# Attention of the later images: values as products with queries on partitions, and whole scan ticks beside it

## The chip, the cores and the metric

The kernel runs on one core of a Trainium2 chip, in float32 throughout. The metric is the device time of one execution in microseconds (us), lower is better. Five instruction streams run side by side on the core, each in its own program order: TensorE (PE in the profile; its weight loads are PEld), VectorE (DVE), ScalarE (ACT), GpSimd (POOL) and the queue that issues DMAs (SP). They wait for each other by semaphores only.

## The reference

Four layers, each added to its input, each on a group-normalised copy of it. `x` has 4 images of 128 channels and 64 x 64 = 4096 pixels.

```
x = x + attention(gn(x))     # q, k, v by 128x128 matrices; softmax over all 4096 pixels
x = x + conv5x5(gn(x))       # weights built from two radial tables
x = x + scan(gn(x))          # two directions: h = exp(delta*A)*h + delta*x*B ; y = C.h + D*x
x = x + conv3x3(gn(x))
```

The part of the attention that the change rewrites is

```
scores = einsum('bic,bjc->bij', q, k) * scale
attn   = softmax(scores, axis=-1)
out    = einsum('bij,bjc->bic', attn, v)
```

The kernel takes the exponential of the scores without subtracting a maximum, sums the exponentials for each query, and divides at the end. If a sum falls out of a wide range a second program with maxima runs; with these inputs it does not run.

## The kernel before, in words

**Two streams of work.** The state-space scan of layer 3 is cut into ticks: `scan_core` has 256 for each image, 1024 in all. A tick handles 128 rows (32 channels by 4 states) over 1024 pixels. Its steps are `drive` (L1387, POOL: input times B, written to `db`), `decay` (L1372, ACT: exp(delta*A) into `da`, which lies in PSUM), `recur` (L1392, DVE: the scan instruction over `da` and `db`; then, on some ticks, the product with C into `hc`), `weigh` (L1418, POOL: that product on the other ticks), `keep` (L1410 and on, ACT: saves the last state) and `collect` (L1423, PE: sums over states into `y`). All else, namely each image's attention, 5x5 convolution, scan operands, and at the end the output convolutions, is a Python generator, `images()`, that issues a few instructions and yields what they are thought to cost.

**What sets the order.** The order is written out at build time. After each half of a tick, a credit grows by half of `PACE` (2.74 us), and the generator is asked for pieces until the credit is spent (L1709 to L1719). So beside the scan of image 0 the front (attention, convolution, operands) of image 1 is issued, and so on; beside the scan of the last image the output convolutions of the first three, at `ENDPACE`. Engines take their instructions in that order and run ahead only within it.

**Half ticks and whole ticks.** PSUM has eight banks. `s`, `a`, `z` and `y` hold one each. Four more are lent either to the pool `s2`, which holds a second score bank and three `da` tiles of 512 columns, or to the pool `wide`, which holds two `da` tiles of 1024. `widen` (L1652) decides: beside a convolution, and at the end, ticks are whole (one decay, one scan, one product with C of 1024 columns); beside attention and operands they are halved (two of each, of 512 columns). `to_pool` (L1329) gives POOL every third product with C in whole ticks and two of five in half ticks beside the attention.

**Attention before.** `attention` (L467) takes blocks of 512 queries, 8 for an image, against 32 tiles of 128 keys: 256 units `u`. In each, `scores` makes one 128x512 score tile in bank `s` or `s2` (keys on partitions), ACT writes its exponential to one of 8 slots of `ring`, and `values`, two units later, multiplies `v` (the weights) with that slot into `acc` (L524), channels on partitions. Once for every four units `sums` (L546) adds the exponentials over keys by four narrow matmuls with ones into `zp`. At a block's end the sums go out to DRAM and back so as to stand as a row on every partition (`spill` to `stage_rows`), and `settle` (L661) multiplies, adds bias and input, and takes a sum for the next normalisation, on DVE. The first image runs without a scan beside it and takes its sums on DVE and POOL instead (`side_sums`).

Of the kernel before, what the change touches and what calls it, by code (L numbers as in the profile page):

```python
# [32 lines left out]
P = 128  # L33
# [3 lines left out]
MM = 512  # L37
# [8 lines left out]
PRODUCT, HOP, SLOT, PACE, ENDPACE, AHEAD = 0.86, 1.7, 0.7, 2.74, 1.5, 4  # L46
# [6 lines left out]
def conv_preact_kernel(  # L53
# [366 lines left out]
    def attention_start(b, xn):  # L420
# [10 lines left out]
        v = v[:, : NJT * C].rearrange("p (j c) -> p j c", c=C)  # L431
# [7 lines left out]
        def keys(i):  # L439

            tag = "saz"[i % 3] if b == 0 else "s" if i < 3 else ("s", "s2")[i % 2]
            pvs[i] = bank(tag, f"pv_{b}_{i}").rearrange("p (t c) -> p t c", c=C)
            for t in range(TPM):
                nc.tensor.matmul(
                    pvs[i][:, t, :], xn[:, bass.ts(i * TPM + t, P)], wv, start=True, stop=True
                )

        def take(i):
            nc.scalar.copy(v[:, i * TPM : (i + 1) * TPM, :], pvs.pop(i))
# [17 lines left out]
    def attention(b, xs, xn, v, st, safe, loads):  # L467

        ring = exchange(b).rearrange("p (r m) -> p r m", m=MM)
        later = {}  # L470
        rq, acc, zp, mb = {}, {}, {}, {}
# [5 lines left out]
        def queries(blk):  # L477
            pr = bank("s", f"pr_{b}_{blk}")
            nc.tensor.matmul(pr, wqk, xn[:, bass.ts(blk, MM)], start=True, stop=True)
            rq[blk] = pools["bg"].tile([P, MM], F32, tag="r", name=f"r_{b}_{blk}")  # L480
            nc.scalar.activation(rq[blk], pr, AF.Identity, bias=bqk)

        def row_max(blk):

            part = small.tile([P, TPM, NM], F32, tag="part", name=f"part_{b}_{blk}")
            for t in range(TPM):
                for k in range(NM):
                    pp = bank("s", f"pmax_{b}_{blk}_{t}_{k}")
                    nc.tensor.matmul(
                        pp, rq[blk][:, bass.ts(t, P)], xn[:, bass.ts(k, MM)],  # L490
                        start=True, stop=True,
                    )
                    nc.vector.tensor_reduce(part[:, t, k : k + 1], pp, AX.X, ALU.max)
            m = small.tile([P, TPM], F32, tag="rmax", name=f"rmax_{b}_{blk}")
            nc.vector.tensor_reduce(m, part, AX.X, ALU.max)
            pb = bank("s", f"pmb_{b}_{blk}")
            spread(pb, m)
            mb[blk] = pools["bg"].tile([P, MM], F32, tag="raw", bufs=1, name=f"mb_{b}_{blk}")
            nc.scalar.copy(mb[blk], pb)

        def spread(dst, cols):

            for t in range(TPM):
                nc.tensor.matmul(
                    dst[:, bass.ts(t, P)], cols[:, t : t + 1].to_broadcast([P, P]), ident,
                    start=True, stop=True,
                )

        def scores(u):
            blk, j = divmod(u, NJT)  # L510
            sc = bank(("s", "s2")[u % 2], f"sc_{b}_{u}")
            nc.tensor.matmul(sc, xn[:, bass.ts(j, P)], rq[blk], start=True, stop=True)  # L512
            pt = ring[:, u % NRING, :]
            if safe:
                nc.vector.tensor_tensor(pt, sc, mb[blk], ALU.subtract)
                nc.scalar.activation(pt, pt, AF.Exp)
            else:
                nc.scalar.activation(pt, sc, AF.Exp)  # L518

        def values(u):  # L520
            blk, j = divmod(u, NJT)
            if j == 0:
                acc[blk] = bank("a", f"acc_{b}_{blk}")
            nc.tensor.matmul(  # L524
                acc[blk], v[:, j, :], ring[:, u % NRING, :], start=j == 0, stop=j == NJT - 1
            )

        due = []  # L530

        def sums_due(u):
            beside = "collected" in ready
            ready.discard("collected")
            if due and due[0][1] <= u and (beside or u >= due[0][2]):
                sums(due.pop(0)[0])
                return PRODUCT
            return 0.0

        def sums(u):  # L540

            blk, j = divmod(u, NJT)
            if j == 3:
                zp[blk] = bank("z", f"zp_{b}_{blk}")
            for g in range(4):
                nc.tensor.matmul(  # L546
                    zp[blk][g * 32 : (g + 1) * 32, :], ones[:, :32],
                    ring[:, (u - 3 + g) % NRING, :], start=j == 3, stop=j == NJT - 1,
                    tile_position=(0, g * 32), skip_group_check=True,
                )  # L550

        state = {}


        fill = pools.get("fill") if not safe else None
        sides = {}
# [11 lines left out]
        def evict_sums(blk):  # L568
            zs = None
            if not fill:  # L570
                zs = pools["bg"].tile([P, MM], F32, tag="zs", bufs=1, name=f"zs_{b}_{blk}")
                nc.scalar.copy(zs, zp.pop(blk))
            elif blk + 1 < NM:
                zs = pools["bg"].tile([P, MM], F32, tag="zs", bufs=1, name=f"zs_{b}_{blk}")
                pz = bank("z", f"pz_{b}_{blk}")
                for g, e in enumerate("dp"):
                    nc.tensor.matmul(
                        pz[g * 32 : (g + 1) * 32, :], ones[:, :32], sides.pop((blk, e)),
                        start=True, stop=True, tile_position=(0, g * 32), skip_group_check=True,
                    )  # L580
                nc.scalar.copy(zs[:64], pz[:64])
            state[blk] = None, zs
# [3 lines left out]
        def spill(blk):  # L586
            raw, zs = state[blk]
            n = 2 if fill else 4
            zd = dram.tile([4, MM], F32, tag="zp", name=f"zd_{b}_{blk}")
            nc.sync.dma_start(zd[:n], zs[0 : n * 32 : 32, :])  # L590
            state[blk] = raw, zd[:n]

        def gather(blk):
            raw, zd = state[blk]
            zt = small.tile([P, 4, RUN], F32, tag="zt", name=f"zt_{b}_{blk}")
            n = zd.shape[0]
            nc.sync.dma_start(zt[:, :n, :], zd.rearrange("g (p j) -> p g j", j=RUN))
            state[blk] = raw, zt[:, :n, :]

        def invert_rows(blk):  # L600
            raw, zt = state[blk]
            z = zall[:, b * NJT + blk * TPM : b * NJT + (blk + 1) * TPM]
            nc.vector.tensor_reduce(z, zt.rearrange("p g j -> p j g"), AX.X, ALU.add)
            zr = small.tile([P, RUN], F32, tag="zr", name=f"zr_{b}_{blk}")
            nc.vector.reciprocal(zr, z)
            state[blk] = raw, zr

        def put_rows(blk):
            raw, zr = state[blk]
            zd = dram.tile([P, RUN], F32, tag="zd", name=f"zi_{b}_{blk}")  # L610
            nc.sync.dma_start(zd, zr)
            state[blk] = raw, zd
# [19 lines left out]
        def turn(blk):  # L632

            raw, zs = state[blk]
            parts = [(zs, zsel)] if zs is not None else [
                (sides.pop((blk, e)), ones[:, 0:1]) for e in "dp"
            ]
            pz = bank("z", f"pz_{b}_{blk}")
            for t in range(TPM):
                for n, (part, add) in enumerate(parts):  # L640
                    nc.tensor.matmul(
                        pz[:, t : t + 1], part[:, bass.ts(t, P)], add,
                        start=n == 0, stop=n == len(parts) - 1,
                    )
            state[blk] = raw, pz

        def invert(blk):
            raw, pz = state[blk]
            z = zall[:, b * NJT + blk * TPM : b * NJT + (blk + 1) * TPM]
            nc.vector.tensor_copy(z, pz[:, :TPM])  # L650
            zr = small.tile([P, TPM], F32, tag="zr", name=f"zr_{b}_{blk}")
            nc.vector.reciprocal(zr, z)
            state[blk] = raw, zr

        def widen_out(blk):
            raw, zr = state[blk]
            pb = bank("z", f"pzb_{b}_{blk}")
            spread(pb, zr)
            state[blk] = raw, pb
# [10 lines left out]

        queries(0)
        ready.add((b, "begun"))
        yield HOP
        HELD = 4
        for u in range(N):
            blk, j = divmod(u, NJT)
            cost = sums_due(u)
            if safe and j == 0:
                row_max(blk)
            scores(u)  # L680
            cost += PRODUCT

            if j == 17 and blk + 1 < NM:
                queries(blk + 1)
                cost += PRODUCT
            w = u - 2
            if w >= 0:
                if w < N - HELD:
                    values(w)
                    cost += PRODUCT  # L690
                d = w % NJT
                if fill:
                    side_sums(w)
                elif d == NJT - 1:
                    sums(w)
                    cost += PRODUCT
                elif d % 4 == 3:
                    due.append((w, u + (3 if d == 3 else 1), u + NRING - 5))
                if d == NJT - 1:
# [9 lines left out]
                    cost += PRODUCT if fill else 0.0  # L709
# [3 lines left out]
            yield cost or HOP  # L713
        for w in (N - 2, N - 1) if fill else ():
            side_sums(w)
        blk = NM - 1

        def taps_to(n):
# [3 lines left out]
            part = kept[:, n * k : min((n + 1) * k, NTAP), :]  # L722
            if not fill and part.shape[1]:
                nc.sync.dma_start(to[:, : part.shape[1], :], part)

        values(N - 4)
        stage_rows(blk - 1, "s")
        yield PRODUCT
# [1072 lines left out]
```

## Time and profile before

| what | value |
|---|---|
| median of 3 runs | 4395.23 us (4394.08 to 4402.77) |
| the profiled execution | 4397.93 us |
| span in its profile, first to last instruction | 4396.1 us |
| busy in the span | PE 3829.8, DVE 3698.7, POOL 3601.9, ACT 2384.6 us |
| first drive of the scan, last drive | 677.4 us, 4322.5 us |

How to read it: the share of the busy time is an average over stages. The page cuts the span into 40 slices of 110 us and gives the busy tenths of each engine:

```profile
PE   8999998999998979999989889999988567575656
PEld 4444433333333333333333333333333112121212
DVE  4832217999998989999989899999989899999996
ACT  3343226666664376666653666666644654545442
POOL 3433308999998979999989899999988799999995
PEclk9999999999999989999999999999999778797877
```

The first six slices are the first image alone; from the seventh on the scan runs. From there to slice 31 three rounds of attention, convolution and operands run beside it, and the last nine slices hold the last image's scan with the output convolutions. A float32 matmul is two passes in the profile, each with a weight load, so counts of PE are twice those of the code. Ends of matmuls are modelled: a pass of 512 columns reads as 592 ns where passes follow each other every 430 ns.

### The profile page before, as it was taken

The page shows a single profiled execution, that of the slowest core. Times are in us where ns is not written, and L with a number is a line of the kernel's source. Part 1 is how long each engine was busy: PE and PEld are TensorE (multiplying, and loading weights), DVE is VectorE, ACT ScalarE, POOL GpSimd, SP SyncE. Part 2 cuts the span into 40 slices and gives each one's busy share as a digit, 9 for nine tenths or more (in the row PEclk, how much of TensorE's full clock was granted, in tenths as well). Part 3 has the DMA queues.
Part 4 walks back from the last instruction along what each step waited for, and adds up shares of the span by engine and source line. Part 5 has one row for each costly group of instructions (what it writes and reads, how often), then busy time and mean ns, then how long its engine had stood idle before and what let it go on. Part 6 is the DMA issues. An engine that isn't in the chain of part 4 may idle for free. (4 is left out here: it accounts for less than half of the span.)

```text
span 4396.1 us, 42164 instructions
## 1 busy us (share of the span) xinstructions
PE 3829.8 (87%) x12828; PEld 1415.9 (32%) x12828; DVE 3698.7 (84%) x3465; ACT 2384.6 (54%) x4331; POOL 3601.9 (82%) x1712
## 2 busy tenths in 40 slices
PE   8999998999998979999989889999988567575656
PEld 4444433333333333333333333333333112121212
DVE  4832217999998989999989899999989899999996
ACT  3343226666664376666653666666644654545442
POOL 3433308999998979999989899999988799999995
PEclk9999999999999989999999999999999778797877
DMA  2120016555555575555555665555555656656562
GB/s 67 45 94 10 3 58 238 184 181 186 176 182 174 180 264 181 178 186 175 181 172 178 213 225 176 194 172 179 173 173 197 237 209 203 226 200 230 181 233 77
DMA packets 241009, 746.40 MB, mean 170 GB/s; under 512 B 44194, under 2 KB 45474, under 8 KB 240516
## 3 DMA queue, kind: packets, MB, share of 16 engines
q1 hardware_dynamic: 238852, 742.88, 49.3%
q8 instruction: 103, 1.69, 0.2%
q14 instruction: 134, 1.10, 0.1%
q10 hardware_dynamic: 1920, 0.73, 0.1%
HBM read 667.82 MB, written 75.69 MB: 169 GB/s over the span
## 5 line engine op out<-in xcount | busy, mean ns | idle before, releaser
L1390 POOL TENSOR_TENSOR db<-dx,br 128x1024 f32<-128x1024 f32 x1024 | 2401.8, 2375 | 225.8 <-DMA dx<-dxd 65.7
L1383 ACT ACTIVATE da<-de,a_neg 128x512 f32<-128x512 f32 (+1 forms) x1635 | 1301.7, 799 | 843.9 <-DVE da L1400 359.2
L512 PE MATMUL sc<-r,x 128*128 128x512 f32 x2048 | 1083.4, 612 | 41.2 <-ACT last L1416 17.1
L524 PE MATMUL acc<-exchange,v 128*128 128x512 f32 x2048 | 1053.5, 596 | 5.2 <-ACT raw L629 1.6
L1421 POOL TENSOR_TENSOR hc<-hc,cr 128x1024 f32<-128x1024 f32 x385 | 914.4, 2375 | 6.5 <-ACT last L1416 4.6
L1403 DVE TENSOR_TENSOR hc<-da,cr 128x512 f32<-128x512 f32 (+1 forms) x1002 | 839.8, 838 | 69.2 <-PE sc L512 1.3
L1400 DVE TENSOR_TENSOR_SCAN da<-da,last,db 128x512 f32<-128x512 f32 (+1 forms) x479 | 859.6, 1795 | 38.0 <-POOL db L1390 28.4
L1439 PE MATMUL y<-hc,sel 128*32 128x512 f32 x4096 | 609.4, 647 | 294.1 <-POOL hc L1421 225.1
L518 ACT ACTIVATE exchange<-sc 128x512 f32<-128x512 f32 x1024 | 601.2, 587 | 394.0 <-PE sc L512 381.2
L512 PEld LDWEIGHTS sc<-r,x 128*128 128x128 f32 x2048 | 362.6, 190 | 648.2 <-issue 357.4
L524 PEld LDWEIGHTS acc<-exchange,v 128*128 128x128 f32 x2048 | 388.2, 191 | 504.7 <-issue 480.2
L1400 DVE TENSOR_TENSOR_SCAN hc<-da,last,db 128x512 f32<-128x512 f32 (+1 forms) x289 | 492.0, 1703 | 8.6 <-POOL db L1390 5.1
L1400 DVE TENSOR_TENSOR_SCAN da<-da,da,db 128x512 f32<-128x512 f32 x363 | 467.0, 1287 | 8.0 <-ACT da L1383 8.0
L566 POOL TENSOR_TENSOR sidep<-sidep,exchange 128x512 f32<-128x512 f32 x120 | 172.0, 1433 | 247.2 <-ACT exchange L518 244.7
L1439 PEld LDWEIGHTS y<-hc,sel 128*32 128x32 f32 x4096 | 114.8, 112 | 734.6 <-POOL hc L1421 316.8
L1400 DVE TENSOR_TENSOR_SCAN hc<-da,hc,db 128x512 f32<-128x512 f32 x248 | 318.1, 1283 | 37.5 <-ACT da L1383 12.9
L566 DVE TENSOR_TENSOR sided<-sided,exchange 128x512 f32<-128x512 f32 x120 | 98.7, 822 | 213.2 <-ACT exchange L518 212.2
L787 PE MATMUL pcm<-xpm,cs 128*128 128x512 f32 x432 | 211.3, 638 | 44.5 <-ACT xpm L392 44.5
L1400 DVE TENSOR_TENSOR_SCAN da<-da,db 128x512 f32<-128x512 f32 (+1 forms) x160 | 240.0, 1500 | 4.5 <-POOL db L1390 2.8
L1416 ACT COPY last<-da 128x1 f32<-128x1 f32 x476 | 73.7, 155 | 275.1 <-DVE hc L1403 273.0
L546 PE MATMUL zp<-exchange,ones 128*32 128x512 f32 x1536 | 205.8, 600 | 0.1
L1039 PE MATMUL pq<-xpe,cs 128*128 128x512 f32 x280 | 134.5, 631 | 39.8 <-ACT xpe L392 39.8
(257 smaller groups left out, 2763.7 us busy)
## 6 DMA issues: line engine op xcount, KB each, us to landing
br<-bm SPq DMA_DIRECT2D x512, 512.0 KB
cr<-cm SPq DMA_DIRECT2D x512, 512.0 KB
de<-dd SPq DMA_DIRECT2D x64, 512.0 KB
dx<-dxd SPq DMA_DIRECT2D x64, 512.0 KB
xs<-in_x_dram SPq DMA_DIRECT2D x16, 512.0 KB
xsd<-xs SPq DMA_DIRECT2D x16, 512.0 KB
xcd<-xc SPq DMA_DIRECT2D x16, 512.0 KB
bm<-bs SPq DMA_DIRECT2D x32, 256.0 KB
```

What stands on the lines that cost most here:

```text
L512: nc.tensor.matmul(sc, xn[:, bass.ts(j, P)], rq[blk], start=True, stop=True)
L518: nc.scalar.activation(pt, sc, AF.Exp)
L524: nc.tensor.matmul(acc[blk], v[:, j, :], ring[:, u % NRING, :], start=j == 0, stop=j == NJT - 1)
L546: nc.tensor.matmul(zp[blk][g * 32 : (g + 1) * 32, :], ones[:, :32], ring[:, (u - 3 + g) % NRING, :], start=j == 3, stop=j == NJT - 1, tile ...
L566: eng.tensor_tensor(s, s, ring[:, u % NRING, :], ALU.add)
L787: nc.tensor.matmul(acc.rearrange("p (r w) -> p r w", w=W), weights[:, t, :], xp[:, y : y + RPM, dx : dx + W], start=t == 0, stop=t == k * ...
L1383: nc.scalar.activation(da, rep["de", b, c, d, g][:, bass.ts(h, size)], AF.Exp, scale=a_neg[:, at(i)])
L1390: nc.gpsimd.tensor_tensor(dbs[i], rep["dx", b, c, d, g], rows["b", b, c, d, q], ALU.mult)
L1400: nc.vector.tensor_tensor_scan(h, da, db[:, cut], before, ALU.mult, ALU.add)
L1403: nc.vector.tensor_tensor(hc[:, cut], h, rows["c", b, c, d, q][:, cut], ALU.mult)
L1421: nc.gpsimd.tensor_tensor(hcs[i], hcs[i], rows["c", b, c, d, q], ALU.mult)
L1439: nc.tensor.matmul(y[r : r + SG, :], sel, hcs[first + gg][:, bass.ts(h, MM)], start=False, stop=q == NQ - 1, tile_position=(0, r), skip_gr ...
```

## The change

The attention of images 1 to 3 is written anew; that of image 0 keeps its way, as `attention_first`.

- **Units.** A unit is now 256 queries by two key tiles: two score matmuls of 256 columns in one bank, one exponential of 512 columns. There are again 256 units for an image, in 16 parts of 256 queries. Score banks are `s` and `z`; `s2` is not used beside attention any more.
- **Values.** The exponentials are the weights (128 keys by 128 queries) and a tile of `v` with a 129th column of ones is what streams: four matmuls of 129 columns for a unit, queries on partitions. The 129th column of `acc` is the sum of the exponentials, so `sums` and the row's way through DRAM go.
- **End of a part.** ACT copies 258 columns out of `acc`, DVE takes reciprocals of two columns, ACT divides two tiles of 128 by a per-partition scale. When two parts are done, `turn` puts the input block into a bank by a product with the identity, adds the four 128x128 tiles turned back by products with the identity, and ACT adds the bias, writes the result and takes its sum.
- **Holding back.** At a part's start `values` of the first unit is held until the second unit's scores are issued (`owed`).
- **Whole ticks.** `widen` goes by a mark `narrow`, set from the end of a convolution to the end of the operands: ticks are whole beside the attention as well.
- **Paces.** 2.65, 2.61, 2.6 and 1.5 for the four images, instead of 2.74 and 1.5; four value matmuls are counted as 0.9.

```diff
-PRODUCT, HOP, SLOT, PACE, ENDPACE, AHEAD = 0.86, 1.7, 0.7, 2.74, 1.5, 4
+PRODUCT, VALUES, HOP, SLOT, AHEAD = 0.86, 0.9, 1.7, 0.7, 4
+PACES = 2.65, 2.61, 2.6, 1.5
...
-        v = v[:, : NJT * C].rearrange("p (j c) -> p j c", c=C)
+        v = v[:, : NJT * (C + 1)].rearrange("p (j c) -> p j c", c=C + 1)
+        nc.gpsimd.memset(v[:, :, C : C + 1], 1.0)
...
+        def scores(u):
+            part, k = divmod(u, NK2)
+            blk, half = divmod(part, 2)
+            cut = bass.ts(half, HM)
+            sc = slots.take("sc")
+            for n in range(2):
+                nc.tensor.matmul(
+                    sc[:, bass.ts(n, HM)], xn[:, bass.ts(2 * k + n, P)], rq[blk][:, cut],
+                    start=True, stop=True,
+                )
+            pt = ring[:, u % NRING, :]
...
+                nc.scalar.activation(pt, sc, AF.Exp)
+
+        def values(u):
+            part, k = divmod(u, NK2)
+            if k == 0:
+                acc[part] = bank("a", f"acc_{b}_{part}")
+            for n in range(2):
+                for t in range(TPH):
+                    nc.tensor.matmul(
+                        acc[part][:, bass.ts(t, CV)],
+                        ring[:, u % NRING, n * HM + t * P : n * HM + (t + 1) * P],
+                        v[:, 2 * k + n, :],
+                        start=(k, n, t) == (0, 0, 0), stop=(k, n) == (NK2 - 1, 1),
+                        skip_group_check=True,
+                    )
+
+        def evict(part):
...
+            nc.scalar.copy(turned[blk][:, cut], acc.pop(part)[:, : TPH * CV])
...
+        def invert(part):
...
+            nc.vector.reciprocal(
+                zall[:, n : n + TPH], rows(blk)[:, half * TPH : (half + 1) * TPH, C]
+            )
+
+        def divide(part):
...
+            for t in range(TPH):
+                row = rows(blk)[:, half * TPH + t, :C]
+                nc.scalar.activation(row, row, AF.Identity, scale=zall[:, n + t : n + t + 1])
+
+        def turn(blk):
+
+            sums[blk] = bank("a", f"po_{b}_{blk}") if blk + 1 == NM else slots.take("po")
+            nc.tensor.matmul(
+                sums[blk], ident, xs[:, bass.ts(blk, MM)], start=True, stop=False,
+                skip_group_check=True,
+            )
+            for t in range(TPM):
+                nc.tensor.matmul(
+                    sums[blk][:, bass.ts(t, P)], rows(blk)[:, t, :C], ident,
+                    start=False, stop=True, skip_group_check=True,
+                )
+            cut = bass.ts(blk, MM)
+            nc.scalar.activation(
+                xs[:, cut], sums.pop(blk), AF.Identity, bias=bv_c, accum_out=st.sum(blk)
+            )
...
+            if u >= 2:
+                owed.append(u - 2)
+            if owed and (owed[0] % NK2 or len(owed) > 1):
+                for w in owed:
+                    values(w)
+                    cost += VALUES
...
-        ready.add((b, "convolved"))
-        ready.discard("convolving")
-        while b > 0 and "wide" in pools:
+        ready.update({(b, "convolved"), "narrow"})
+        while "wide" in pools:
             yield HOP
...
+        ready.discard("narrow")
         ready.add((b, "all"))
...
-                wide = (B - 1, "all") in ready or "convolving" in ready
+                wide = "narrow" not in ready
...
-                if b + 1 == B:
-                    pace = ENDPACE
+                pace = PACES[min(b, len(PACES) - 1)]
```

## The prediction

> **What bounds the kernel now.** The page's chain of waits covers 1% of the span (the last 70 us), so I read in another order: the slices, then busy time by stage, then each engine's own rows and waits in the attention stage. In the slices PE, DVE and POOL all stand near 9 from the eighth slice to the thirty-first; only stages tell which one decides. A stage is cut where the drives (L1390, one a tick) and the attention's matmuls begin and end. Busy time of PE, PEld, DVE, ACT, POOL in the attentions of images 1, 2, 3, in one convolution stage, and beside the last scan:
>
> ```profile
> 723.00:1370.00 647.00, 620.08 (x2300) 223.84 (x2299) 612.54 (x641) 421.80 (x866) 605.41 (x270) 0.99 0.55 185
> 1640.00:2292.00 652.00, 625.91 (x2306) 224.17 (x2305) 615.04 (x643) 423.50 (x872) 602.94 (x267) 0.99 0.54 181
> 2564.00:3218.00 654.00, 624.50 (x2306) 225.09 (x2305) 615.68 (x647) 422.19 (x871) 603.05 (x268) 0.99 0.53 179
> 1370.00:1540.00 170.00, 163.69 (x524) 63.71 (x522) 161.96 (x114) 66.23 (x76) 162.64 (x75) 0.99 0.51 174
> 3496.00:4250.00 754.00, 476.01 (x1503) 144.20 (x1504) 725.36 (x428) 359.26 (x576) 717.06 (x327) 0.79 0.61 214
> ```
>
> The built order has 184 drives in each attention (9 to 193, 262 to 446, 515 to 699), so a tick takes 647/184 = 3.52, 3.54 and 3.55 us. The last stage has nearly the same scan in whole ticks; its drives:
>
> ```profile
> L1390 POOL TENSOR_TENSOR db<-dx,br x255: 2337/2372/2452, 3495.3 to 4317.9; 128x1024 f32<-128x1024 f32 x128
> ```
>
> That is 822.6/254 = 3.24 us a tick. What VectorE runs in a tick, half ticks in the first attention and whole ones in the last stage (count, busy, mean, idle before):
>
> ```profile
> L1403 DVE TENSOR_TENSOR hc<-da,cr 128x512 f32<-128x512 f32 x220 | 152.1, 691 | 14.1 <-PE sc L512 0.4 <-PE acc L524 0.4
> L1400 DVE TENSOR_TENSOR_SCAN da<-da,da,db 128x512 f32<-128x512 f32 x110 | 141.5, 1286 | 0.0
> L664 DVE TENSOR_TENSOR rz<-raw,rz 128x512 f32<-128x512 f32 x7 | 4.8, 680 | 0.0
> ```
> ```profile
> L1400 DVE TENSOR_TENSOR_SCAN da<-da,last,db 128x1024 f32<-128x1024 f32 x112 | 262.2, 2341 | 9.7 <-POOL db L1390 9.7
> L1403 DVE TENSOR_TENSOR hc<-da,cr 128x1024 f32<-128x1024 f32 x156 | 191.0, 1224 | 15.0 <-issue 0.4
> ```
>
> And who VectorE and ScalarE waited for in the first attention:
>
> ```profile
> DVE pzb L664 <- PE pzb L504: 4.7, 1, 4.7
> DVE da L1400 <- ACT da L1383: 2.1, 1, 2.1
> ```
> ```profile
> ACT da L1383 <- DVE da L1400: 119.6, 91, 2.6
> ACT da L1383 <- DVE hc L1400: 50.9, 76, 1.0
> ACT exchange L518 <- PE sc L512: 29.1, 35, 2.8
> ```
>
> VectorE waits for others about 12 us in 647; the other 22 of its 34 idle us are about 0.035 us between each two of 641 instructions. ScalarE waits 170 us for VectorE to free decays. So VectorE sets the attention tick. PE is not full, whatever its 96% says: by pitches (0.43 us a 512-column pass, below) 512 score, 512 value, 128 sum and 184 y pass-times make (512+512+128+184) x 0.43 + 6 for queries = 580 of 647 us, 90%.
>
> **What the Trainium skill says.** "TensorE: Matmul & The Clock Gate", "LDWEIGHTS (loading the stationary operand)", prices a load at its columns over 1.2, 107 ns for 128, and says loads are pulled ahead of running matmuls. This is the point on which the changed products stand: 128 new weights for each 129 columns. The first image's values have that very shape:
>
> ```profile
> L444 PE MATMUL pv<-wv,x x47: 274/275/341, 21.8 to 27.0; 128*128 128x128 f32 x47
> ```
>
> 47 passes begin within 5.2 us: 0.113 us each, with loads whose rows read 0.192 us. The load is hidden. The same page ("What's actually happening") says the idle array runs at half clock; the trace agrees in that the earlier passes of that group stand 0.213 us apart. In the attention the granted clock is 0.99. "ScalarE: Activation LUTs", "What ACT_TABLE_LOAD costs", gives 186 ns + 0.833 ns an element, 93 ns more for a per-partition operand; its 612 ns for a 512 copy stand beside 0.59 measured, so I use it for shapes that the trace lacks. "PSUM — Partial Sum Buffer", "Terms", says that one starting matmul clears the written flags of its whole bank; the two query tiles in one accumulator rest on it, and no run here shows it.
>
> **The change part by part, per later image.**
>
> 1. Ticks become whole beside the attention (widen, L1652): the order of the changed kernel has them from tick 10, 262, 516 and 772, half ticks only in 242-262, 497-516, 753-772. VectorE before: 220 half products x 0.691 + 368 half scans (1.21 to 1.29, in all 467 us) + about 15 us of settle and statistics = 3.33 us a tick, 3.52 with the gaps. After: a scan 541.6/233 = 2.324 (the four whole-scan rows of the last stage) and 2/3 x 1.224 = 0.816: 3.14; 1.8 instructions x 0.037 of gap 0.07; waits as in the last stage, 12.4/233 = 0.05: 3.26.
>
> 2. POOL's share of products falls from 2/5 to 1/3 (to_pool, L1329): 1.333 x 2.35 = 3.13 a tick, and 31.4/232 = 0.135 of idle before drives (mostly DMA) in the last stage: 3.27. So POOL stands level with VectorE.
>
> 3. Values (L524) and sums (L546) go; 1024 matmuls of 129 columns come. 2 x 1024 x 0.113 = 231 us against (512 + 128) x 0.43 = 275. Scores are the same columns in halves: 0.218 a 256-column pass (between 0.113 and 0.43), 1024 x 0.218 = 223 against 220. The turn back (L754, L759 of the changed kernel) adds 8 x (0.86 + 4 x 0.226) = 14, the old turn and widening leave 2. Over 180 ticks with y (0.43) and queries: 1.28 + 1.24 + 0.08 + 0.43 + 0.04 = 3.07 us a tick, 93% of 3.28.
>
> 4. Settle leaves VectorE (8 x (0.68 + 0.75 + 0.34) = 14 us), 16 reciprocals of about 0.18 come, 0.02 a tick. The row's way through DRAM (28 DMAs on SP) goes; nothing waited for it, so nothing.
>
> 5. ScalarE: out go, per block, copies of accumulator, sums and row (0.59 + 0.58 + 0.60); in come two copies of 258 (0.40 each, estimate), four divisions of 128 (0.39, estimate), one add with accumulator (0.67 + 0.19): +1.45 us a block, 12 us an image. One whole decay (1.117) replaces two halves (0.691). Per tick 1.12 + 0.16 + 1.42 x 0.59 + 0.21 = 2.33 of 3.28 us: cover is there. The price is order: ScalarE now waits for VectorE once a whole tick, and exponentials (two score banks) queue behind that wait. PE can run about one unit (score and value, 1.77 us) past the last exponential; the wait, copy and decay hold ScalarE up to about 2 us. PE has 0.2 us a tick to lose. Below, this costs 0 if PE's lateness absorbs it (a decay needed a tick later leaves about 1.9 us of play), above, PE's whole slack and more; I take 0.01 to 0.02.
>
> 6. One accumulator bank for 16 parts instead of 8: the first values of a part are held back for a second score (owed list), 1.7 us for a copy of 0.40. Before, PE's two rows lost about 1 us at each of 24 evictions; I take no change.
>
> The tick is 3.29. Attention has 180, 180 and 182 ticks before the order turns to convolutions (10-190, 262-442, 516-698): 540 (two taken off for ends) x 3.29 = 1777 against 647 + 652 + 654 = 1953: **-176**. Fewer ticks and lower paces (2.65, 2.61, 2.6 for 2.74) leave more ticks to the convolutions: 164 for 154. They took 170 + 173 + 174 = 517; VectorE and POOL hold 94 to 96% there, so the rate falls only from 3.36 to 3.30: 541, **+24**. The operand stages keep their work and get 5 ticks more (58 for 53), between 0 and 3.24 us each: **+9**. One more half tick at the start: **+4**. The last scan has 251 ticks left instead of 255: **-13**. The first image and the 74 us after the last drive stay. Sum **-152**: profiled run 4397.9 to 4246, and as that run lies 2.7 us above the median, 4243 for a median.
>
> **The rivals.**
> A. As above, VectorE and POOL at 3.22 to 3.36: 4206 to 4281. For it: VectorE hardly waits now, and the last stage shows the rate. 65%.
> B. ScalarE's longer wait starves PE, or PE with y bursts (1.74 us every four ticks) becomes the bound. At 3.45 a tick 540 x 0.16 = 86 more: 4330; at most break-even. For it: three engines within 7%. Against: whole ticks beside convolutions run at 3.36 with PE at 96%, though there exponentials are absent. 21%.
> C. Slower: the weights do not hide in value products. They read the ring that ScalarE fills, and the accumulator begins at odd columns. At 0.19 a pass PE needs 3.07 + 2048 x 0.077/180 = 3.95 a tick, +356: 4600. It decides from 0.16 a pass, where the tick is 3.57 and the gain gone. Against: the 0.113 above. 6%.
> D. The change gives more than that, because VectorE's gaps and POOL's DMA waits shrink: tick 3.19, 4190. 5%.
> E. Whole ticks win nothing since the split to POOL only shifts work; then PE's relief alone (0.09 us a tick, hidden) shows: no change. 3%.
>
> **How the numbers follow.** Forecast 4243. The range 4195 to 4325 leaves out C, E, half of B's upper part and the end of D, some 20%. What this measurement can tell from no change is about 0.2%, 9 us. Faster: A, D and nearly all of B, 0.91; same: E, 0.03; slower: C, 0.06.
>
> **What would show it.** Right: drives in the attentions 3.2 to 3.36 us apart, VectorE rows of 1024 elements with little idle, value passes 0.113 us apart, PE waits for exponentials of well under 0.2 us a tick. Wrong: VectorE idle before scans for decays (B, by ScalarE), value passes near 0.19 (C), or convolution stages that give back far more than 24 us.

## The result, and the profile after

| | median, us | runs | ratio to before |
|---|---|---|---|
| before | 4397.06 | 4394.08 to 4402.77 | |
| after | 4357.14 | 4352.88 to 4359.47 | 0.9907 [0.9889, 0.9924] |

The change brings 40 us where 152 were forecast; 4357 lies above the range (4195 to 4325). The span fell from 4396.1 to 4351.1 us. The stages of both profiled executions, from drive to drive, with the ticks issued in them:

| stage | before | forecast | after |
|---|---|---|---|
| three attentions | 1951.9 (552 ticks) | 1777 (540) | 1854.2 (540) |
| three convolutions | 519.0 (154) | 541 (164) | 557.6 (164) |
| operand stages | 301.2 (53) | 310 (58) | 317.9 (58) |
| start | 45.7 (9) | 50 (10) | 50.3 (10) |
| last scan | 827.1 (255) | 814 (251) | 821.3 (251) |

Every stage got the ticks that were counted for it. Of the 109 us missing in these rows, 77 are in the attentions: 3.43 us a tick, not 3.29. The windows of the kernel after, in the order of those shown of before (length, then busy time of PE, PEld, DVE, ACT, POOL, then PE's clock, the DMA share, GB/s):

```profile
727.00:1339.00 612.00, 572.52 (x3861) 459.83 (x3859) 549.14 (x325) 385.15 (x706) 553.53 (x241) 0.99 0.53 181
1628.00:2248.00 620.00, 578.26 (x3875) 463.33 (x3874) 557.80 (x331) 392.59 (x718) 560.20 (x243) 0.99 0.53 183
2542.00:3162.00 620.00, 574.77 (x3876) 460.07 (x3875) 560.91 (x335) 393.31 (x719) 564.68 (x246) 0.99 0.53 184
1340.00:1520.00 180.00, 168.07 (x528) 65.55 (x528) 172.40 (x120) 75.19 (x90) 175.33 (x84) 0.96 0.56 190
3457.00:4200.00 743.00, 465.54 (x1481) 143.84 (x1482) 709.19 (x418) 354.62 (x571) 703.00 (x321) 0.80 0.61 208
```

VectorE did get the lighter work: 549 to 561 us busy, after 612 to 616. But in each attention it now stands idle for about 60 us, and so does POOL, so that no engine is full. A bound of before has gone and nothing took its place as a bound: it must be waits. VectorE's waits in the second attention of the kernel after (waiting line, releaser, us in total, times, longest):

```profile
DVE da L1475 <- ACT da L1458: 45.1, 34, 4.0
DVE da L1475 <- POOL db L1465: 1.8, 2, 1.4
```

One group: scans that wait for their decay, 34 times in some 180 ticks, 1.3 us each. Over the three attentions it is 104 times and 131 us. A wait that comes with a fixed price and not on every tick has a pattern; a few ticks of VectorE's timeline show it (start, duration, what, idle before):

```profile
1797.72 1.23 DVE L1478 TENSOR_TENSOR hc<-da,cr 128x1024 f32<-128x1024 f32 x1
1798.86 2.29 DVE L1475 TENSOR_TENSOR_SCAN da<-da,db 128x1024 f32<-128x1024 f32 x1
1801.24 1.23 DVE L1478 TENSOR_TENSOR hc<-da,cr 128x1024 f32<-128x1024 f32 x1
1802.38 2.28 DVE L1475 TENSOR_TENSOR_SCAN hc<-da,db 128x1024 f32<-128x1024 f32 x1
1805.92 2.30 DVE L1475 TENSOR_TENSOR_SCAN da<-da,db 128x1024 f32<-128x1024 f32 x1 [1.25 <-ACT da L1458]
1808.31 1.22 DVE L1478 TENSOR_TENSOR hc<-da,cr 128x1024 f32<-128x1024 f32 x1
```

The scan at 1802.38 writes to `hc`, not `da`: it is a tick whose product is POOL's, so that VectorE goes straight to the next scan. That one finds no decay. ScalarE's timeline in the same stretch says why:

```profile
1799.17 1.12 ACT L1458 ACTIVATE da<-de,a_neg 128x1024 f32<-128x1024 f32 x1
1801.39 0.60 ACT L709 ACTIVATE exchange<-sc 128x512 f32<-128x512 f32 x1 [1.09 <-PE sc L696]
1802.50 0.16 ACT L1491 COPY last<-da 128x1 f32<-128x1 f32 x1 [0.52 <-DVE hc L1478]
1804.70 1.12 ACT L1458 ACTIVATE da<-de,a_neg 128x1024 f32<-128x1024 f32 x1 [2.04 <-DVE hc L1475]
1805.76 1.06 ACT L709 ACTIVATE exchange<-sc 128x512 f32<-128x512 f32 x2
```

ScalarE has stood still for 2.04 us before the decay at 1804.70, and what released it is the end of the very scan that ran just ahead (1802.38 + 2.28). With two decay tiles it ought to wait for the scan, product and saved state of the tick before that one, which were over at 1802.66 (the copy at L1491). It did not, because it is given the *same* tile as the tick ahead of it. The addresses in the built program confirm this: in the three attentions 38, 34 and 33 of the 540 ticks lie in the same PSUM banks as the tick before, always the tick after one of POOL's; in the convolutions and the last stage 0 or 1, and in the kernel before 2 of its 413 whole ticks. In the second attention ScalarE stands still before a decay for a scan 31 times (first line). Exponentials wait behind the decay, hence the pair at 1805.76, and PE behind those (second line):

```profile
ACT da L1458 <- DVE hc L1475: 61.7, 31, 2.1
```
```profile
PE sc L696 <- ACT exchange L709: 31.3, 32, 2.6
```

### The profile page after: what moved, and what is told of

Its sections match the earlier page's. It is cut to its first block, busy times and chain, and to the rows that moved or that the text cites. A ratio compares the mean times of both kernels' runs of the same rounds, so it can differ in the third digit from the quotient of the medians.

```text
span 4351.1 us, 49535 instructions
## 1 busy us (share of the span) xinstructions
PE 3707.9 (85%) x17628; PEld 2145.4 (49%) x17628; DVE 3568.5 (82%) x2554; ACT 2319.0 (53%) x3910; POOL 3531.0 (81%) x1683
## 5 line engine op out<-in xcount | busy, mean ns | idle before, releaser
L1458 ACT ACTIVATE da<-de,a_neg 128x1024 f32<-128x1024 f32 (+1 forms) x1091 | 1162.9, 1067 | 586.2 <-DVE hc L1478 274.0
L1475 DVE TENSOR_TENSOR_SCAN da<-da,last,db 128x1024 f32<-128x1024 f32 (+1 forms) x501 | 1151.0, 2297 | 120.9 <-ACT da L1458 83.1
L696 PE MATMUL sc<-r,x 128*128 128x256 f32 x3072 | 817.9, 391 | 107.8 <-ACT exchange L709 94.4
L1478 DVE TENSOR_TENSOR hc<-da,cr 128x1024 f32<-128x1024 f32 (+1 forms) x708 | 828.9, 1171 | 63.4 <-DVE da L1475 1.8
L717 PEld LDWEIGHTS acc<-v,exchange 128*128 128x128 f32 x6144 | 808.6, 193 | 49.2 <-issue 10.1
L717 PE MATMUL acc<-v,exchange 128*128 128x129 f32 x6144 | 811.9, 277 | 1.9 <-ACT exchange L709 1.9
L1475 DVE TENSOR_TENSOR_SCAN hc<-da,last,db 128x1024 f32<-128x1024 f32 (+1 forms) x267 | 596.2, 2233 | 4.8 <-POOL db L1465 4.3
L1475 DVE TENSOR_TENSOR_SCAN da<-da,db 128x1024 f32<-128x1024 f32 (+1 forms) x171 | 377.2, 2206 | 52.5 <-ACT da L1458 44.7
L1491 ACT COPY last<-da 128x1 f32<-128x1 f32 x512 | 81.0, 158 | 594.5 <-DVE hc L1478 593.5
L506 PE MATMUL acc<-exchange,v 128*128 128x512 f32 x512 | 261.9, 594 | 0.9
L499 PE MATMUL sc<-r,x 128*128 128x512 f32 x512 | 262.0, 594 | 0.6 <-ACT r L482 0.6
```

The costliest lines, as they stand in the source:

```text
L506: nc.tensor.matmul(acc[blk], v[:, j, :C], ring[:, u % NRING, :], start=j == 0, stop=j == NJT - 1)
L696: nc.tensor.matmul(sc[:, bass.ts(n, HM)], xn[:, bass.ts(2 * k + n, P)], rq[blk][:, cut], start=True, stop=True,)
L717: nc.tensor.matmul(acc[part][:, bass.ts(t, CV)], ring[:, u % NRING, n * HM + t * P : n * HM + (t + 1) * P], v[:, 2 * k + n, :], start=(k, ...
L1458: nc.scalar.activation(da, rep["de", b, c, d, g][:, bass.ts(h, size)], AF.Exp, scale=a_neg[:, at(i)])
L1475: nc.vector.tensor_tensor_scan(h, da, db[:, cut], before, ALU.mult, ALU.add)
L1478: nc.vector.tensor_tensor(hc[:, cut], h, rows["c", b, c, d, q][:, cut], ALU.mult)
```

## Experiments

**Theories.** *Same bank*: the two decay tiles, taken from a pool under one tag, do not alternate beside the attention, and each tick in the banks of the one ahead costs VectorE about a decay. *Order on ScalarE* (rival B of the prediction): decays are late because they are queued among exponentials, and so is PE; which tile a decay gets is of no weight. *Whole ticks win nothing* (rival E): what was gained is PE's relief.

**e1: the tiles alternate.** Each tick's tile is fixed by its parity; nothing else changes: in the built programs of the kernel after, e1 and e2 every engine has the same instructions in the same order, and only the addresses of the decays, with the waits that follow from them, differ.

```diff
-                pools["wide"].tile([P, CH], F32, tag="da", bufs=2, name=f"pl{n}_{b}_{c}")
+                pools["wide"].tile([P, CH], F32, tag=f"da{n}", bufs=1, name=f"pl{n}_{b}_{c}")
...
-            da = pool.tile([P, size], F32, tag="da", bufs=2 if size == CH else 3, name=f"da_{i}_{h}")
+            tag, bufs = (f"da{i % 2}", 1) if size == CH else ("da", 3)
+            da = pool.tile([P, size], F32, tag=tag, bufs=bufs, name=f"da_{i}_{h}")
```

> The changed kernel with the two whole-tick decay tiles bound to two fixed tags, even ticks in one pair of banks and odd ticks in the other (and the last convolution's use of the same banks by the same tags). Nothing else. Theory 1 (banks): in the three attentions 105 of 542 ticks get the very banks of the tick before, each of them right after a tick whose product with C is POOL's; their decay cannot start before the scan ahead of them has ended, and VectorE then idles for a decay, some 1.2 us. With alternate banks VectorE's waits for decays in the attentions fall from about 130 us to under 25, the tick from 3.43 to 3.25-3.32, the time to 4240-4285. Theory 2 (order): ScalarE's exponentials and PE hold each other up through the order of ScalarE's queue, whatever the banks; the time stays within 10 us of 4357.

Measured: 4240.8 us (4238.38 to 4244.88), ratio to before 0.9648 [0.9635, 0.9661]. The three attentions fell from 1854.2 to 1743.7 us, with the same 540 ticks; the other stages stayed within 1.5 us (convolutions 557.5, operands 318.6, last scan 819.8). So 110.5 us for 105 same-bank ticks: 1.05 us each. The windows of the attentions:

```profile
727.00:1298.00 571.00, 562.55 (x3864) 455.86 (x3862) 546.46 (x325) 390.78 (x707) 551.42 (x242) 1.00 0.56 195
1588.00:2171.00 583.00, 566.06 (x3874) 458.53 (x3874) 555.07 (x330) 397.60 (x718) 557.66 (x244) 0.99 0.56 194
2466.00:3053.00 587.00, 568.51 (x3874) 458.62 (x3874) 559.00 (x335) 396.01 (x718) 561.58 (x246) 0.99 0.56 193
```

Busy times are within some 2% of those of after; what went is idle time. Waits of this kernel in the first attention:

```profile
DVE da L1476 <- ACT da L1459: 5.6, 6, 1.8
DVE da L1476 <- POOL db L1466: 5.3, 4, 2.3
```
```profile
PE sc L696 <- ACT exchange L709: 1.1, 1, 1.1
```

Where the kernel after has 46.4 us of waits for decays in that stretch, 5.6 are left (23.6 of 131 over the three), and of PE's 29.7 us of waits for exponentials 1.1: they followed from the tile, not from the order. No decay of that stretch is released by a scan any more. The same three ticks (product, product, POOL's) now run without a break:

```profile
1703.92 2.29 DVE L1476 TENSOR_TENSOR_SCAN da<-da,db 128x1024 f32<-128x1024 f32 x1
1706.31 1.23 DVE L1479 TENSOR_TENSOR hc<-da,cr 128x1024 f32<-128x1024 f32 x1
1707.45 2.28 DVE L1476 TENSOR_TENSOR_SCAN hc<-da,db 128x1024 f32<-128x1024 f32 x1
1709.65 2.30 DVE L1476 TENSOR_TENSOR_SCAN da<-da,db 128x1024 f32<-128x1024 f32 x1
```

**e2: the suspected cost, more of it.** The tiles are fixed as in e1, except that every tick after one of POOL's, in attentions and convolutions, stays in the tile of the tick ahead: 181 in the attentions (76 more than after) and 51 in the convolutions.

```diff
-        pooled = {}
+        pooled, turn_of = {}, {}
...
-            da = pool.tile([P, size], F32, tag="da", bufs=2 if size == CH else 3, name=f"da_{i}_{h}")
+            stay = i > 0 and (i - 1) % 3 == 2 and "narrow" not in ready and (B - 1, "all") not in ready
+            turn_of[i] = turn_of.get(i - 1, 0) ^ (not stay)
+            tag, bufs = (f"da{int(turn_of[i])}", 1) if size == CH else ("da", 3)
+            da = pool.tile([P, size], F32, tag=tag, bufs=bufs, name=f"da_{i}_{h}")
```

> The same fixed tags, but every tick after a POOL tick takes the banks of the tick before, in all of the attentions (181 ticks instead of 105) and in the convolution stages (51 instead of 1). Theory 1: 76 more ticks in the attentions and 50 in the convolutions at 0.8 to 1.25 us: 4357 + 100 to 155, that is 4450 to 4520. Theory 2: within 15 us of 4357.

Measured: 4505.82 us (4502.95 to 4508.81), ratio 1.0251 [1.0236, 1.0267]: slower than before the change. Attentions 1956.9 us, which is 102.7 over after for the 76 more (1.35 us each); convolutions 607.9, which is 50.3 for 50 more (1.0 each), where the kernel after had one. The first attention's waits:

```profile
DVE da L1478 <- ACT da L1461: 72.3, 56, 2.1
```
```profile
ACT da L1461 <- DVE hc L1478: 99.7, 52, 2.1
```

The second line is the mark of it in a profile: a decay released by a scan, at nearly every third tick.

**e4: the shared tag, but another engine saves the state.** After a tick whose product is VectorE's, the last reader of the decay tile is the copy of one column in `keep` (ScalarE, L1491), behind that product and often behind exponentials. After one of POOL's ticks it is the scan itself. With that copy on VectorE, right behind the product:

```diff
-                nc.scalar.copy(last[b][:, at(i)], end)
+                nc.vector.tensor_copy(last[b][:, at(i)], end)
```

> The changed kernel with its two decay tiles under one tag as it is, but the copy that keeps a tick's last state (128x1) goes to VectorE instead of ScalarE. In the built program no tick then takes the banks of the tick before. Theory 1 (banks), with the copy on ScalarE as what held the older bank longest: VectorE's waits for decays go as in e1; VectorE has a short copy more in 7 of 8 ticks, 0.06 to 0.15 us each with its gap, so the attentions stand at 3.28 to 3.38 a tick and the time at 4290 to 4350. If the copy has nothing to do with the choice of banks or the banks nothing with the time, VectorE's waits stay and the time is 4400 to 4480 (4357 and the copies).

Measured: 4286.96 us (4284.67 to 4291.3), ratio 0.9749 [0.9733, 0.9766]. Under the shared tag no tick has the banks of the one ahead any more, and attentions take 1783.6 us. The time is 3 us below the range written for it. The waits for decays that are left in the first attention:

```profile
DVE da L1475 <- ACT da L1458: 3.1, 2, 1.8
```

e1 is 46 us faster. What e4 has more are the copies, in VectorE's stream, one in nearly every tick of an attention (count, busy, mean, idle before):

```profile
L1491 DVE COPY last<-da 128x1 f32<-128x1 f32 x118 | 17.3, 147 | 0.0
L1491 DVE COPY last<-hc 128x1 f32<-128x1 f32 x59 | 9.0, 153 | 1.8
```

26 us of rows in this attention, some 79 in three; the attentions are 40 us longer than in e1, and the last scan, where they run too, 11 us. That the copies cost all of this was not tried apart. So a late reader of a tile is what goes together with the wrong choice; *how* the pool comes to choose (my reading: it takes the tile that comes free first in the order as it is built, and that is the one just used by POOL's tick) was only argued.

**e3: half ticks beside the attention, the rest as after.** This leaves the value products, the freed engines and the lower paces, without whole ticks.

```diff
         ready.add((b, "attended"))
+        ready.discard("narrow")
...
-        ready.discard("narrow")
+        if b + 1 == B:
+            ready.discard("narrow")
         ready.add((b, "all"))
```

> The changed kernel with half ticks beside the attentions, as before the change: values as products with queries on partitions alone. VectorE's own sum for a half tick without settle: (612.5 - 12)/184 = 3.26 busy, 0.12 of gaps and 0.04 of waits: 3.42 a tick. Theory 1: 180 x 3.42 = 616 us an attention, as long as in the changed kernel (613 to 621), so 4345 to 4370: whole ticks then bring nothing as they are placed. Theory 2 also gives about this, if the hold-up comes from whole ticks; if it comes from the value products themselves (PE), the attentions stay at 3.5 or above and the time is 4385 or more.

Measured: 4354.42 us (4348.52 to 4355.55), ratio 0.9903 [0.9888, 0.9918]: the time of the kernel after. Its windows of the attentions:

```profile
727.00:1335.00 608.00, 574.42 (x3822) 455.11 (x3814) 576.67 (x596) 410.42 (x879) 578.39 (x253) 0.99 0.53 183
1625.00:2248.00 623.00, 578.94 (x3866) 461.51 (x3864) 588.49 (x606) 417.65 (x893) 585.57 (x255) 0.99 0.52 182
2544.00:3165.00 621.00, 579.55 (x3886) 460.83 (x3882) 592.34 (x615) 422.48 (x900) 590.95 (x258) 0.99 0.53 184
```

The same length as after by another way: VectorE busier by 27 to 31 us an attention, in nearly twice the instructions, but hardly waiting for decays (17 us in three). All of the change's 40 us is therefore had without whole ticks: the new value products with what they take off VectorE and PE, and the lower paces, which e3 keeps; how much each of these brings was not tried. With tiles that alternate, whole ticks are worth 114 us more (e3 to e1), and in the kernel after the repeated tile takes back 116 (e1 to after).

**e5: e1 at the old paces.** Is it right to issue more ticks beside the attentions?

```diff
-PACES = 2.65, 2.61, 2.6, 1.5
+PACES = 2.74, 2.74, 2.74, 1.5
```

> e1 with the paces of before (2.74 for the first three images, 1.5 for the last). The fronts then end 33 ticks earlier (attentions 516 ticks, convolutions 156, last scan 287). If the lower paces cost time in the convolution stages because they add ticks there, these fall from 557 to about 525; the attentions stay at 3.23 to 3.30 a tick if PE (then 3.16 of products a tick) has room, 4235 to 4265 in all. If PE is the next bound, the attentions go to 3.35 or more and the time to 4280 or more.

Measured: 4277.51 us (4275.38 to 4279.23), ratio 0.9729 [0.9713, 0.9745], 37 us behind e1. Attentions 1708.4 us for 517 ticks (e1 1743.7 for 540), convolutions 538.1 for 156 ticks, but the last scan is left with 287 ticks and 935.2 us (819.8 in e1). In the first attention:

```profile
720.00:1300.00 580.00, 566.48 (x3854) 459.65 (x3853) 541.32 (x322) 392.35 (x706) 550.19 (x244) 0.99 0.55 191
```

Less VectorE work in the same length: a tick is 3.28 to 3.33 us there, not 3.21 to 3.24. With fewer ticks offered, VectorE and POOL idle while PE is the nearest to full (566 of 580 us). Of PE's 13.5 us of idle time in these 580 us, 9.3 are one wait of the next stage:

```profile
PE pq L1113 <- ACT xpe L393: 9.3, 1, 9.3
```

So PE stands still for some 4 us of this attention, and 23 ticks fewer shorten the three attentions by only 35 us, 1.5 us a tick; the products for scores and values stay the same. Neither range written for this run held: 4277.5 lies between them, nearer to PE as the next bound, and the convolutions fell to 538 us, not to about 525. The lower paces of the change are right: the 36 ticks that e1 puts beside other work cost some 78 us there (115 less the 37 of the whole) and save 115 at the end.

## Why the prediction was wrong

The step that failed is the last term of step 1: "waits as in the last stage, 12.4/233 = 0.05". It took for granted that whole ticks beside an attention would take turns on the two tiles as they do in the last stage and the convolutions. They do not: 105 of 540 ticks get the tile of the tick ahead, and the term measured 131/540 = 0.24 us a tick for decays alone. e1, which changes the tile and nothing else, makes the attentions 110.5 us shorter; e2, which repeats the tile after every tick of POOL's, pays for it again, also in the convolutions, where it was all but absent.

Rival B named the symptom rightly, "VectorE idle before scans for decays", at 4330, and gave it the wrong cause: ScalarE's order and starved exponentials. e1 keeps that order and the waits go. PE's waits for exponentials in the trace of the kernel after were an effect of the tile. Step 5 named the place ("ScalarE now waits for VectorE once a whole tick, and exponentials queue behind that wait") but priced it at 0.01 to 0.02, on the ground that "a decay needed a tick later leaves about 1.9 us of play". After one of POOL's ticks the repeated tile leaves no play: the decay can only start when the scan ahead has ended, and VectorE needs it at once. The built order alone tells which tile each decay gets, and so held the repetition before any run. Rival C falls: see step 3 below. Rival E saw rightly that whole ticks win nothing in the kernel as changed (e3 and after are 3 us apart), but not why: with alternating tiles they win 114.

The other terms, by what the trace of e1 shows, where the waits no longer cover them:

- *Step 1, the whole tick on VectorE*: 2.324 for the scan held in e1's first attention (413.6/178), the product too (144.5/178 = 0.81), but the gap of 0.07 is not there on balance: in e1's lines above the product starts 0.10 us after the scan's row, and the next scan 0.09 us before the product's row has ended. Busy time, in which what overlaps counts once, is 546.46/178 = 3.07 us a tick, not 3.21. The trace of before had this already: the rows summed in step 1 make (152 + 467 + 15)/184 = 3.45, not 3.33; 3.33 is the busy time, 612.5/184. VectorE then has about 0.14 of idle, not 0.05: 3.21 to 3.24 in all, against 3.26.
- *Step 2, POOL level with VectorE*: 551.42/178 = 3.10 busy beside 3.07. Right.
- *Step 3, the value products*: the weights hide. Eight of them in the kernel after (durations min/median/max, first and last start):

```profile
L717 PEld LDWEIGHTS acc<-v,exchange x8: 190/192/193, 1801.0 to 1801.9; 128*128 128x128 f32 x8
L717 PE MATMUL acc<-v,exchange x8: 273/275/277, 1801.2 to 1802.0; 128*128 128x129 f32 x8
```

  Seven steps in 0.8 us, about 0.11 a pass where 0.113 was taken from the first image's products; rows of loads read 0.192 as they did there. The load price in the Trainium skill's "TensorE: Matmul & The Clock Gate", "LDWEIGHTS (loading the stationary operand)", of 107 ns for 128 columns, fits these steps of 0.11 us, each with a new load; the loads' own rows are longer than it.

  PE's sum as a whole was too low: in e1's first attention PE is busy 562.55/178 = 3.16 us a tick, not 3.07, and waits 5.5 us in all. That is 98% of the stretch where 93% was written. Once the tiles alternate, PE is nearest to full, before POOL (97%) and VectorE (96%); which of its terms was too small was not taken apart.
- *Step 4*: settle has left VectorE's rows. Its 14 us an image, on the engine that was the bound, is about the 40 us that e3 shows for all but the whole ticks; rival E had put that part at nothing. Settle, value products and paces were not tried apart, so that this is an agreement of sizes, not a cause shown.
- *Step 5, the prices*: divisions 0.397 us for an estimate of 0.39, copies of 258 columns 0.369 for 0.40 (count, busy, mean ns, idle before):

```profile
L749 ACT ACTIVATE turned<-turned,zall 128x128 f32<-128x128 f32 x32 | 11.1, 397 | 8.0 <-DVE zall L740 8.0
L732 ACT COPY turned<-acc 128x258 f32<-128x258 f32 x16 | 5.9, 369 | 0.7 <-PE acc L717 0.6
```

- *Step 6, one accumulator bank*: in the first attention of the kernel after PE's value products (L717) waited 0.5 us in all, for an exponential, never for the copy out of `acc`. No cost, as taken.
- *Convolutions*: 557.6 us, not 541. The 164 ticks are right, but the rate stayed at 3.40 us a tick where 3.30 was expected. Operand stages: 317.9, not 310, so the five ticks more cost 16.7/5 = 3.3 us each, all exposed, the upper end that was written beside the 9.

That e1 ends at 4240.8, by the forecast of 4243, is in part luck, since misses offset each other: its attentions are 33 us shorter than forecast, the convolutions, operands and last scan 31 longer.

## What to carry to other kernels

"Two buffers" is not "alternating buffers": where a pool chooses the tile and consumers end on different engines, the next writer can be given the tile just read, and then waits for the one instruction it was meant to overlap. Before costing a double-buffered wait, follow the addresses in the built order through each kind of iteration, here the one in three whose product goes elsewhere; in a profile, the mark is a producer released by the consumer that runs immediately ahead. When work falls on every engine and the time hardly does, look for a wait with a fixed price and a period before calling another engine the bound.

## What the runs showed of the hardware that was not expected

Rows of VectorE instructions overlap: after a whole product (1.23 us as the trace has it) the next scan starts 1.14 us after the product did, as at 1706.31 and 1707.45 in e1. Gaps taken from a stage of many short rows did not carry over. And a copy of one column, 128x1, costs VectorE 0.147 us and ScalarE 0.16: small as it is, one a tick on the fuller engine went with 40 us more in the attentions of e4 than in those of e1.
